# An account of VectorE and GpSimd in a kernel's planner, half-sized GpSimd sums, last divisors on TensorE, a norm in halves

## The chip, the cores and the metric

One Trainium2 chip, one of its cores. The metric is the device time of one execution in microseconds (us), lower is better. TensorE multiplies matrices (PE in the profile; PEld are its weight loads), VectorE (DVE), ScalarE (ACT) and GpSimd (POOL) work on rows of 128 partitions, and SyncE (SP) issues most DMAs. Each engine runs its own instructions strictly in the order in which the program lists them, and waits at an instruction until the semaphores that it names have been raised. So the order of the list is the schedule.

## The reference

Four images of 256 channels and 48 by 48 pixels, all float32. Two layers, each added to its input:

```
x = x + proj(attention(qkv(relu(batchnorm(conv3x3(groupnorm(x)))))))        # 8 heads of 32, 2304 tokens
g = groupnorm(x)
w = conv3x3(g) -> 45 maps; softmax over each 9            # 5 dilations x 9 taps
cat = [g] + [sum over taps k of shift(g, d, k) * w[d, k]  for d in (1, 6, 12, 24, 36)]
x = x + batchnorm over all images (conv1x1(cat))
```

## The kernel before

The images are handled one after the other, in stages that alternate.

**Attention** of image b (`attention`, L1268): nine units of 512 queries (the ninth takes the last 256 queries of both halves of the heads), each in 18 steps of 128 keys. In a step TensorE makes the scores of four heads (`scores`), ScalarE takes their exponent into p, TensorE multiplies p with v into `num` (`weigh`, L1310), and VectorE adds p to `acc` (L1340). Steps in LENT lend three quarters of that sum to a GpSimd-queued DMA that adds into `extra`, which lies in `ring`; L1347 adds `extra` to `acc`. At a unit's end `close` (L1360) makes the divisors: `sums` (L1352) multiplies `acc` with ones on TensorE into `den`, VectorE transposes, takes reciprocals, transposes back and multiplies into `ao` (L1367 to L1377). For the ninth unit nothing follows that could hide it.

**The mixed stage** after it does the second layer of image b (`dynamic_filters`, L1431) and the convolution and q, k, v of image b+1 (`conv_qkv` with `conv_blocks`, L1071) side by side. First `project` (L1407) multiplies `ao` into `pp` and adds it to the image in `pad`; then come the group norm's statistics, and the norm of the whole image: one half of the channels on VectorE (L641), one on ScalarE (L1963). Then these streams run:

- the filters: TensorE makes the 45 maps `pg`, softmax runs over them (`weights`, L1478), and they go out to HBM by DMA and come back in two layouts;
- `near` (L1724), dilation 1, for six chunks c of 384 pixels: nine times ScalarE brings a map into PSUM (`wb`), VectorE multiplies it with the shifted image (`prod`, L1754), and GpSimd adds the product to `near` (L1759), 128x768 at a time;
- `far` (L1585), the other four dilations, as matmuls: VectorE builds a matrix `amat` by predicated copies (L1648, L1660), TensorE multiplies it with the transposed image into two PSUM banks, three times a chunk, and ScalarE or VectorE takes these out, whichever `moved` (L1459) finds less loaded;
- `mixes` (L1809), the 1x1 convolution `py` of all that, chunk by chunk;
- `other`, the convolution of the next image as a Winograd scheme along both axes: GpSimd makes the transformed inputs in `Blocks` (L951: `sum`, `stage0`, `rest`, `along`), TensorE multiplies (`pc`, L1139), and ScalarE, VectorE and GpSimd combine the results; sums with both inputs in SBUF go to VectorE or GpSimd as `either` (L1062) decides. After it come q, k (`pq`) and v (`pv`).

The order of all that is found while the program is written out: `Clock` (L692) keeps a time for each engine, each step adds its assumed cost to it, and `drive` (L1918) takes the first stream whose due time has come by the clock of TensorE, or else a piece of `other`. So a changed cost in the clock changes the order of the instructions on all engines, and which engine gets a sum. What the chip does is not asked.

After attention of the fourth image the second layer has no convolution beside it; there `other` is `late` (L1869), two chunks of the third image that were put off, and the outputs' end (`finish`, L2037).

Of the kernel before, what the change touches and what calls it, by code (L numbers as in the profile page):

```python
# [8 lines left out]
F32 = mybir.dt.float32  # L9
# [48 lines left out]
def conv_preact_kernel(  # L58
# [487 lines left out]
    with tc.tile_pool(name="w", bufs=1) as wpool, tc.tile_pool(  # L546
# [145 lines left out]
        class Clock:  # L692
# [3 lines left out]
            def __init__(self):  # L696
                self.t = dict.fromkeys(("PE", "DVE", "ACT", "POOL"), 0.0)

            def __call__(self, engine, ns, *after):

                self.t[engine] = max(self.t[engine], *(a + 150.0 for a in after), 0.0) + ns
                return self.t[engine]

# [247 lines left out]
        class Blocks:  # L951
# [28 lines left out]
            def sum(self, out, x, y, op):  # L980
                nc.gpsimd.tensor_tensor(out, x, y, op)
                return clock("POOL", 2800)

            def stage0(self):
# [3 lines left out]
                nc.scalar.mul(v[5], d[1], 4.0)  # L988
                self.sum(v[0], d[4], v[0], ALU.subtract)
# [11 lines left out]
            def rest(self):  # L1001
# [3 lines left out]
                for out, x, y, op in (  # L1005
                    (3, d[4], d[2], ALU.subtract), (6, v[6], v[4], ALU.subtract),
                    (4, v[3], v[6], ALU.subtract), (3, v[3], v[6], ALU.add),
                ):
                    yield room
                    end = self.sum(v[out], x, y, op)  # L1010
# [51 lines left out]
        def either(out, a, c, op, *after):  # L1062

            part = 0.5 if len(out.shape) == 2 and out.shape[-1] == XN else 1.0
            if clock.t["POOL"] + 1400 * part <= clock.t["DVE"] + 1000 * part:
                nc.gpsimd.tensor_tensor(out, a, c, op)
                return clock("POOL", 1400 * part, *after)
            nc.vector.tensor_tensor(out, a, c, op)
            return clock("DVE", 1000 * part, *after)

        def conv_blocks(b, psum_tile, blocks, pool, hid):  # L1071
# [23 lines left out]
            def before(i, o):  # L1095

                s12, d12, s34, d34 = (blocks.held[:, j, o] for j in range(4))
                if i == 0:
                    t = spare.pop(0)
                    axpy(t, s34, -4.0, s12)  # L1100
                    relu(o, 2, t, clock("DVE", 700))
                    either(s12, s12, s34, ALU.subtract)
                elif i == 5:
                    t = spare.pop(0)
                    axpy(t, d34, -2.0, d12)
                    relu(o, 1, t, clock("DVE", 700))
                    axpy(d12, d34, -8.0, d12)
                    clock("DVE", 700)
# [159 lines left out]
        def attention(b, q, k_, vT, pools, spare, project, scratch, following):  # L1268
# [41 lines left out]
            def weigh(u, m, p):  # L1310
# [21 lines left out]
                if end and m == NT - 1:  # L1332
                    sums(u, p, True, False)
# [11 lines left out]
                if u and m == (NT - 3 if end else NT - 1):  # L1345
# [6 lines left out]
            def sums(u, rhs, start, stop):  # L1352
                if start:
                    state[u]["den"] = three(f"den_{b}_{u}")[:, 0, :]
                for j, r in enumerate(heads):
# [4 lines left out]
            def close(u):  # L1360

                sums(u, state[u]["acc"], u < last, True)
                if u == last and b == B - 1:
# [18 lines left out]
            for i, (u, m) in enumerate(steps):  # L1382
# [10 lines left out]
                if m == 6 and (u % NH == 1 or u == last):  # L1393
                    while (chunk + 1) * CH <= units[u if u == last else u - 1][0][1]:
                        pp = three(f"pp_{b}_{chunk}")
                        if spare:
# [10 lines left out]
        def project(b, c, ao, pp, norm):  # L1407

            t = pads[b % 2]
            for o in range(NH):  # L1410
                for g in range(NH):
                    nc.tensor.matmul(
                        pp[:, o, :CH],
# [5 lines left out]
            for o in range(NH):  # L1419
                x1 = inside(t, o, c * R, R)  # L1420
                nc.vector.scalar_tensor_tensor(
                    out=x1, in0=rows_of(pp[:, o, :CH]), scalar=pbias[:, o : o + 1], in1=x1,
# [8 lines left out]
        def dynamic_filters(b, ao, chunk, norm, other, pools):  # L1431
# [27 lines left out]
            def moved(dst, src, size, *after, slow=1.0):  # L1459

                if clock.t["ACT"] <= clock.t["DVE"]:
                    nc.scalar.copy(dst, src)  # L1462
                    return clock("ACT", 180 + 0.83 * slow * size, *after)
                nc.vector.tensor_copy(dst, src)
                return clock("DVE", 160 + 1.04 * slow * size, *after)
# [4 lines left out]
            for t in (lg, bmat, amat):  # L1470
                nc.gpsimd.memset(t, 0.0)
# [6 lines left out]
            def weights(cs):  # L1478

                c, pair = cs[0], len(cs) == 2  # L1480
                pg = misc(f"pg_{b}_{c}")
# [58 lines left out]
                yield clock("DVE", 1100 if pair else 320) + 150  # L1540
# [44 lines left out]
            def far():  # L1585

                for c in range(NCK):
# [8 lines left out]
                    for h in range(NH):  # L1596
# [6 lines left out]
                            slow=1.9,  # L1603
                        ))
# [52 lines left out]
                    rowsof = bmat.rearrange("p a (n y) x -> p (a n) y x", y=3)  # L1657
                    for t in range(3):
                        yield lambda: clock.t["DVE"] - AHEAD
# [9 lines left out]
                        end = clock("DVE", 1060)  # L1669
# [54 lines left out]
            def near():  # L1724

                for number, (c, k) in enumerate(sent):
# [32 lines left out]
                    nc.gpsimd.tensor_tensor(cat, cat, prod, ALU.add)  # L1759
                    end = clock("POOL", 1800, end)  # L1760
# [190 lines left out]
            while chunk < NCK:  # L1951
                project(b, chunk, ao, ps_y.tile([P, 2, 512], F32, tag="y", name=f"pp_{b}_{chunk}"), norm)
# [5 lines left out]
            table(AF.Exp)  # L1958
            norm.shift_of()
            for h in range(NH):  # L1960
                t = inside(gn, h)
                if h:
# [415 lines left out]
```

## Time and profile before

| | us |
|---|---|
| median of 3 runs | 2768.17 (2763.59 to 2770.75) |
| the profiled execution | 2768.08 |
| its span, first to last instruction | 2766.3 |

Of the span TensorE is busy 94%, VectorE 77%, ScalarE 65%, GpSimd 27%. By stage, from the busy time in windows of the trace:

| stage, us from the start | length | PE busy | DVE busy | ACT busy | POOL busy |
|---|---|---|---|---|---|
| first convolution, 0 to 152 | 152 | 127.0 | 101.9 | 64.8 | 49.7 |
| attention, four times (the first: 152 to 519) | 367 | 362.1 | 323.4 | 321.7 | 30.9 |
| mixed stage of image 0, 519 to 819 | 300 | 276.6 | 198.8 | 119.5 | 158.6 |
| mixed stage of image 1, 1186 to 1487 | 301 | 278.8 | 195.7 | 119.4 | 158.5 |
| mixed stage of image 2, 1858 to 2132 | 274 | 248.2 | 195.5 | 116.2 | 162.9 |
| last stage, 2502 to 2766 | 264 | 213.9 | 154.6 | 94.7 | 88.5 |

In the lines of the timeline below, the columns are start (us from the span's start), duration (us), engine, line of the kernel, operation, out<-in, shape, count; in brackets the engine's idle time before it and what ended that.

### The profile page before, as it was taken

The numbers are of one execution on the slowest core, as the hardware profiler recorded it, in microseconds if no ns is written. First come the engines' busy times: TensorE is split into PE (matmuls) and PEld (weight loads), VectorE is DVE, ScalarE is ACT, GpSimd is POOL, SyncE is SP. The second block draws the span as 40 slices with busy tenths as digits, with TensorE's granted clock in tenths as the row PEclk, the third lists the DMA queues.
The fourth block names the chain that finished last, engine by engine and source line by source line (L and its number), as shares of the span: only waits on it lengthen the run. The fifth ranks groups of instructions, "written<-read, shape, count | busy, mean of one in ns | idle before, by whom it ended". The sixth has DMA issues, their size and how long they took to land. (4 is left out here: it accounts for less than half of the span.)

```text
span 2766.3 us, 42026 instructions
## 1 busy us (share of the span) xinstructions
PE 2596.0 (94%) x16820; PEld 1089.6 (39%) x16820; DVE 2142.2 (77%) x2045; ACT 1796.7 (65%) x2242; POOL 741.7 (27%) x641
## 2 busy tenths in 40 slices
PE   6999999889999999988999999998999999999994
PEld 5632222455562222345554222244555222234452
DVE  7778888777739988858765988885876988885476
ACT  3478888633449988843346888883445988873244
POOL 5200100456420100065550001016654010000352
PEclk9999999999999999999999999999999999999997
DMA  4704444323242444422333444442335344442465
GB/s 172 219 18 98 109 98 103 81 69 99 78 92 58 105 99 95 109 77 76 89 70 67 92 98 102 99 94 71 86 83 133 93 93 100 94 92 63 118 180 183
DMA packets 135979, 273.64 MB, mean 99 GB/s; under 512 B 56040, under 2 KB 97936, under 8 KB 134880
## 3 DMA queue, kind: packets, MB, share of 16 engines
q0 software_dynamic: 25952, 135.74, 21.5%
q1 hardware_dynamic: 109824, 135.14, 18.4%
q8 instruction: 134, 2.20, 0.4%
q14 instruction: 69, 0.57, 0.1%
HBM read 112.12 MB, written 36.04 MB: 54 GB/s over the span
## 5 line engine op out<-in xcount | busy, mean ns | idle before, releaser
L1340 DVE TENSOR_TENSOR acc<-acc,p 128x2048 f32<-128x2048 f32 (+1 forms) x572 | 1061.2, 1855 | 122.7 <-ACT p L1304 73.1
L1304 ACT ACTIVATE p<-se 128x1536 f32<-128x1536 f32 x648 | 938.7, 1449 | 0.1
L1295 PE MATMUL so<-q,k 32*128 32x512 f32 (+1 forms) x1440 | 726.4, 592 | 19.6 <-ACT p L1303 18.9
L1295 PE MATMUL se<-q,k 32*128 32x512 f32 (+1 forms) x4320 | 735.0, 592 | 0.0
L1324 PE MATMUL num<-p,vT 128*32 128x512 f32 (+1 forms) x5760 | 706.2, 560 | 4.6 <-ACT p L1304 2.4
L1303 ACT ACTIVATE p<-so 128x512 f32<-128x512 f32 x648 | 388.4, 599 | 193.8 <-PE se L1295 82.8
L1759 POOL TENSOR_TENSOR near<-near,prod 128x768 f32<-128x768 f32 x192 | 351.8, 1833 | 357.2 <-DVE prod L1754 347.6
L1295 PEld LDWEIGHTS so<-q,k 32*128 32x128 f32 x1440 | 216.1, 183 | 535.0 <-ACT p L1303 496.3
L1324 PEld LDWEIGHTS num<-p,vT 128*32 128x32 f32 x5760 | 134.5, 108 | 479.2 <-issue 444.3
L1344 POOL DMA_DIRECT2D ring<-p x124 | 105.5, 851 | 779.8 <-ACT p L1304 464.8
L1754 DVE TENSOR_TENSOR prod<-wb,pad 128x768 f32<-128x768 f32 x192 | 181.7, 953 | 68.5 <-ACT wb L1741 48.9
L1854 PE MATMUL py<-far,wsc 128*128 128x384 f32 x704 | 234.5, 487 | 0.0
L1295 PEld LDWEIGHTS se<-q,k 32*128 32x128 f32 x4320 | 226.7, 183 | 5.4 <-ACT p L1304 4.1
L1741 ACT COPY wb<-ws 128x384 f32<-128x384 f32 x216 | 109.0, 509 | 174.7 <-DVE prod L1754 146.4
L1462 ACT COPY far<-far 128x512 f32<-128x512 f32 x92 | 97.4, 1105 | 143.4 <-PE far L1688 142.0
L1342 POOL DMA_DIRECT2D ring<-p x32 | 17.9, 558 | 640.8 <-ACT p L1304 481.5
L1854 PEld LDWEIGHTS py<-far,wsc 128*128 128x128 f32 x704 | 131.9, 190 | 89.8 <-issue 1.8
L1489 PE MATMUL pg<-pad,wcat 128*45 128x384 f32 x864 | 151.7, 498 | 3.5 <-ACT lg L1547 2.1
L1219 PE MATMUL pq<-hid,wqkv 128*128 128x384 f32 x384 | 130.2, 497 | 7.6 <-ACT hid L1089 5.4
L1688 PE MATMUL far<-amat,xT 64*128 64x256 f32 x576 | 86.0, 416 | 18.3 <-DVE amat L1660 18.3
L1219 PEld LDWEIGHTS pq<-hid,wqkv 128*128 128x128 f32 x384 | 73.6, 194 | 60.6 <-ACT hid L1089 7.0
L1340 DVE TENSOR_TENSOR acc<-p,p 128x2048 f32<-128x2048 f32 x36 | 82.3, 2285 | 19.6 <-ACT p L1304 19.6
(305 smaller groups left out, 2711.1 us busy)
## 6 DMA issues: line engine op xcount, KB each, us to landing
ring<-p POOLq DMA_DIRECT2D x156, 768.0 KB, 5.7
ws<-w_d SPq DMA_DIRECT2D x216, 192.0 KB
ring<-u_d SPq DMA_DIRECT2D x36, 512.0 KB
pad<-in_x SPq DMA_DIRECT2D x14, 1152.0 KB
xst<-in_x POOLq DMA_DIRECT2D x36, 192.0 KB, 3.6
x_d<-pad SPq DMA_DIRECT2D x36, 192.0 KB
u_d<-pad SPq DMA_DIRECT2D x12, 512.0 KB
y_d<-y SPq DMA_DIRECT2D x14, 384.0 KB
```

Of the source, the lines that this page charges most:

```text
L1219: nc.tensor.matmul(pq[:, :CH], wqkv[:, i, s, g * P : (g + 1) * P], hid[:, i, cols], start=(i == 0), stop=(i == NH - 1),)
L1295: nc.tensor.matmul(dst[:, at : at + n], k_[r, g, m * P : (m + 1) * P], q[r, g, q0 : q0 + n], start=True, stop=True,)
L1303: nc.scalar.activation(p[:, 0, :], s1, AF.Exp, scale=QS)
L1304: nc.scalar.activation(p[:, 1:, :], s3, AF.Exp, scale=QS)
L1324: nc.tensor.matmul(st["num"][r, at : at + n], vT[:, m, g * P + j * D : g * P + (j + 1) * D], p[:, j, at : at + n], start=(m == 0 and not s ...
L1340: nc.vector.tensor_tensor(st["acc"][:, js], other[:, js], p[:, js], ALU.add)
L1344: nc.gpsimd.dma_start(out=extra, in_=p[:, 1:], accum_op=ALU.add)
L1489: nc.tensor.matmul(pg[64 * s : 64 * s + NG, :CH], wcat[:, ii, k, :], shifted(ii, cc, k // 3 - 1, k % 3 - 1), start=(i == 0 and k == 0), st ...
L1741: nc.scalar.copy(pw[:, :CH], fetched[c, k][0])
L1754: nc.vector.tensor_tensor(prod.rearrange("p h (r w) -> p h r w", w=WW), wb, src, ALU.mult)
L1759: nc.gpsimd.tensor_tensor(cat, cat, prod, ALU.add)
L1854: nc.tensor.matmul(py[c][:, o, :CH], wsc[:, n * NH + i, o * P : (o + 1) * P], rhs, start=(n == 0 and i == 0), stop=(n == order[-1] and i = ...
```

## The change

- `Clock` gets an account of sums: it remembers when GpSimd's recorded work runs, `both` books a VectorE instruction that reads two SBUF operands so that it starts when the GpSimd instruction running then has ended and pushes later GpSimd work back, and `alone` gives that start without booking. `either`, the predicated copies of `amat`, the softmax's last product, the convolution's `axpy` and the copy of `own` use it, with other costs (a sum of 128x576: GpSimd 1300 and VectorE 900 instead of 1400 and 1000). The due time between the three copies of `amat` goes: they follow each other.
- GpSimd's sums of `Blocks` and of `near` are made in halves, one for each half of the channels: 128x600 and 128x384 instead of 128x1200 and 128x768.
- `stage0` gets a sum that stood in `rest`: v3 = d4 - d2, now first of all.
- The ninth unit's divisors: VectorE's last two sums (L1347, and L1340 for step 16) go. In step 16 TensorE adds p, `acc` and `extra` into `den` by 11 matmuls, in step 17 p by four. Five matmuls without use (`busy`) follow in each of the four attentions; before, they stood in the last one alone.
- `lg`, `bmat`, `amat` are cleared by VectorE instead of GpSimd.
- The norm after `project` is made in two halves of 24 rows, with 900 ns of `other` by the clock between them; the exponential's table is loaded in `weights` of chunk 0 instead of before the norm.
- In the last stage `pp` lies in two single banks of the pool `k`, not in the double bank of the pool `y`.

In the built program the number of instructions on TensorE grows by 43 (15 warm, 28 for the divisors); 14 copies out of the far banks go from VectorE to ScalarE (92 and 52 before, 106 and 38 after); in the three mixed stages together TensorE's order, VectorE's and GpSimd's differ in most places from the first chunk on.

```diff
 class Clock:
     def __call__(self, engine, ns, *after):
-        self.t[engine] = max(self.t[engine], *(a + 150.0 for a in after), 0.0) + ns
+        at = max(self.t[engine], *(a + 150.0 for a in after), 0.0)
+        if engine == "POOL":
+            if self.held[0] <= at < self.held[1]:
+                at = self.held[1]
+            self.sums = self.sums[-40:] + [(at, at + ns)]
+        self.t[engine] = at + ns
         return self.t[engine]
+    def alone(self, *after):
+        at = max(self.t["DVE"], *(a + 150.0 for a in after), 0.0)
+        return next((end for start, end in self.sums if start <= at < end), at)
+    def both(self, ns, *after):
+        at = self.alone(*after)
+        self.t["DVE"] = at + ns
+        self.held = at, at + ns
+        if any(start >= at for start, end in self.sums):
+            self.sums = [(start + ns, end + ns) if start >= at else (start, end)
+                         for start, end in self.sums]
+            self.t["POOL"] += ns
+        return self.t["DVE"]
...
 def sum(self, out, x, y, op):
-    nc.gpsimd.tensor_tensor(out, x, y, op)
-    return clock("POOL", 2800)
+    for h in range(NH):
+        nc.gpsimd.tensor_tensor(out[:, h], x[:, h], y[:, h], op)
+        end = clock("POOL", 1400)
+    return end
 def stage0(self):
...
+    self.sum(v[3], d[4], d[2], ALU.subtract)
     self.sum(v[0], d[4], v[0], ALU.subtract)
...
 def either(out, a, c, op, *after):
-    if clock.t["POOL"] + 1400 * part <= clock.t["DVE"] + 1000 * part:
+    if clock.t["POOL"] + 1300 * part <= clock.alone(*after) + 900 * part:
...
-    return clock("DVE", 1000 * part, *after)
+    return clock.both(900 * part, *after)
...
 def weigh(u, m, p):
...
-    if end and m == NT - 1:
-        sums(u, p, True, False)
+    if end and m >= NT - 2:
+        sums(u, p, m == NT - 2, m == NT - 1)
+        if m == NT - 2:
+            sums(u, state[u]["acc"], False, False)
+            sums(u, extra, False, False, 1)
...
-    if u and m == (NT - 3 if end else NT - 1):
+    if u and m == NT - 1 and not end:
         nc.vector.tensor_tensor(rest, rest, extra, ALU.add)
 def close(u):
-    sums(u, state[u]["acc"], u < last, True)
-    if u == last and b == B - 1:
+    if u < last:
+        sums(u, state[u]["acc"], True, True)
+    else:
         busy(ps_a.tile([P, 512], F32, tag="one", name="warm"), 5)
...
 for t in (lg, bmat, amat):
-    nc.gpsimd.memset(t, 0.0)
+    nc.vector.memset(t, 0.0)
...
+    yield lambda: clock.t["DVE"] - AHEAD
     for t in range(3):
-        yield lambda: clock.t["DVE"] - AHEAD
         nc.vector.copy_predicated(amat, ...)
-        end = clock("DVE", 1060)
+        end = clock.both(1060)
...
-    nc.gpsimd.tensor_tensor(cat, cat, prod, ALU.add)
-    end = clock("POOL", 1800, end)
+    for h in range(NH):
+        nc.gpsimd.tensor_tensor(cat[:, h], cat[:, h], prod[:, h], ALU.add)
+        end = clock("POOL", 920, end)
...
-table(AF.Exp)
 norm.shift_of()
-for h in range(NH):
-    t = inside(gn, h)
+for part in range(2):
+    for h in range(NH):
+        t = inside(gn, h, HH // 2 * part, HH // 2)
...
-run(2500)
+    run((900, 1600)[part])
```

## The prediction

> **What bounds the kernel now.** I read the page's first part, then busy time in windows for each stage, then TensorE's waits in one mixed stage, then the timeline. TensorE is busy 94% of the span. In windows of the first mixed stage and of the last stage (window, length, then busy us with instruction counts for PE, PEld, DVE, ACT, POOL, then clock, DMA share, GB/s):
>
> ```profile
> 519.00:819.00 300.00, 276.63 (x1214) 163.37 (x1210) 198.84 (x256) 119.49 (x207) 158.57 (x94) 0.98 0.34 84
> 2502.00:2766.00 264.00, 213.88 (x952) 114.92 (x944) 154.61 (x219) 94.70 (x142) 88.54 (x51) 0.92 0.46 139
> ```
>
> No other engine is full there, so a mixed stage lasts as long as TensorE's work and the waits in it: 23.4, 22.2 and 25.8 us idle in the three. The waits of 519 to 819 (waiting instruction, releaser, then sum, count, mean):
>
> ```profile
> PE far L1688 <- DVE amat L1660: 6.1, 1, 6.1
> PE pc L1139 <- ACT one L1154: 2.9, 1, 2.9
> PE pp L1412 <- DVE ao L1377: 2.8, 1, 2.8
> PE xa L1608 <- ACT own L1462: 2.4, 4, 1.2
> PE xa L1608 <- DVE own L1464: 2.4, 1, 2.4
> PE py L1854 <- POOL near L1759: 1.5, 1, 1.5
> PE den L1356 <- DVE acc L1340: 1.3, 1, 1.3
> ```
>
> The largest comes from sums that exclude each other:
>
> ```profile
> 578.87 3.03 POOL L981 TENSOR_TENSOR cv_q<-pad,cv_q 128x1200 f32<-128x1200 f32 x1
> 579.56 2.95 DVE L1068 TENSOR_TENSOR cv_v<-cv_q,cv_v 128x576 f32<-128x576 f32 x1
> ...
> 582.44 2.96 DVE L1068 TENSOR_TENSOR two<-one,two 128x288 f32<-128x288 f32 x1
> 585.32 1.00 DVE L1660 COPY_PREDICATED amat<-along_y,bmat 128x768 f32<-128x768 uint32 x1
> 586.37 2.08 PE L1688 MATMUL far<-amat,xT 64*128 64x256 f32 x8 [6.10 <-DVE amat L1660]
> ```
>
> A 128x288 sum that takes 0.45 us at its shortest takes 2.96 beside a GpSimd sum of 3 us; four such stand ahead of the third copy of `amat`. After attention the other waits follow:
>
> ```profile
> 524.42 1.06 PE L1356 MATMUL den<-acc,ones 128*32 128x512 f32 x8 [1.33 <-DVE acc L1340]
> 528.24 4.51 PE L1412 MATMUL pp<-ao,wp 128*128 128x384 f32 x8 [2.75 <-DVE ao L1377]
> 533.33 4.12 PE L1139 MATMUL pc<-cv_v,ring 128*128 128x288 f32 x14 [0.58 <-POOL cv_v L1057]
> 543.47 1.72 PE L1139 MATMUL pc<-cv_v,ring 128*128 128x288 f32 x6 [2.92 <-ACT one L1154]
> ```
>
> And in the last stage:
>
> ```profile
> 2509.75 2.82 PE L1412 MATMUL pp<-ao,wp 128*128 128x384 f32 x8 [0.40 <-DVE ao L1377]
> 2514.50 5.16 PE L1881 MATMUL pl<-pad,wsc 128*128 128x384 f32 x10 [1.93 <-issue]
> 2577.30 0.88 PE L1638 MATMUL wT<-ident,wq 36*64 36x36 f32 x12 [2.21 <-DMA wq<-w_d]
> ```
>
> **What the Trainium skill says.** "SBUF — State Buffer", "Who interferes with whom": a VectorE instruction with two SBUF inputs and a GpSimd instruction that reads SBUF shut each other out for the whole instruction. The trace agrees (0.45 against 2.96 us). "TensorE: Matmul & The Clock Gate", "What's actually happening": after an idle window the clock is half, until TensorE has been busy some 3.4 us. The trace agrees: the same eight pp matmuls take 4.51 us in the first stage, 5.46 in the second, 2.82 in the last, which has the five warm matmuls. "Perfetto Trace Analysis", "GPSIMD Engine Instruction": spans on GpSimd are rough; so I take spacing where I can: five near sums start within 9.40 us, 1.88 each. "VectorE: DVE Perf Modes", "Zero memsets can be issued as uint32 (trn2)": a memset takes a cycle per element; at 0.96 GHz, which that page states too, the 1440 elements of lg, bmat, amat give an estimate of 1.5 us. No memset on VectorE is in the trace of before.
>
> **The change, part by part.** Sums against the profiled 2768.08 us (span 2766.3, 1.8 around it); the median of the runs is 2768.17, no correction.
>
> *Divisors.* After 519.09 TensorE would run six sets of four 32-row matmuls, 0.87 us each (num 16; den from p 16, from acc, from extra; num 17; den from p 17): done at 524.3, transposes from 524.5 where they now start at 525.55. So 1.0 us earlier in stages 1 and 2; 0.5 in stage 3 and 0.1 in the last, where p 17 itself comes later. VectorE loses 1.76 + 2.29 us. No new wait: acc of step 15 was ready at 520.18, extra long before.
>
> *Warm.* The five matmuls lie in the idle time before pp (2.75 us). pp falls from 4.51 and 5.46 to 2.82, but the next pc waits for GpSimd anyway (0.58 us at 533.33, and the wait grows by what pp gains). By itself worth about nothing; it makes GpSimd the bound of this spot.
>
> *GpSimd's start.* v3 = d4 - d2 needs only pad, whose readers end with the last scores at 519.2; its first half can run before 522. The next sums are now shut out by VectorE's L1340 until 524.4; without it they start near 522.8. The memsets leave GpSimd (1.5 us) for VectorE's idle time before pp, 4.75 us long, which covers them; uncovered they would cost pp 1.5 us. Neither v3 nor the memsets issue a DMA; on GpSimd's queue they pass only one another. First pc at about 531.4 instead of 533.33: -1.9 us in each mixed stage.
>
> *Norm in halves, table load moved.* Now ScalarE loads the table (1.28 us at 539.43), then norms 2304 elements (2.30 us from 540.84), and `one` queues behind it; TensorE resumes at 543.47 after 2.92 us. With the load gone and half a norm first, `one` comes near 539.1 and TensorE resumes near 539.6: 3.9 us earlier, of which 1.9 are counted above, so -2.0. The table load goes ahead of chunk 0's exponent, beside the 12 pg matmuls and convolution; cover ample. If ScalarE's second half then delays the next copy, I lose up to 1.15 us of it.
>
> *far.* With the account, VectorE's sums stand clear of GpSimd's, which are half as long (1200 elements now 2.52 us unblocked), and the three copies are adjacent. The 6.1 us wait goes; so does the slow clock behind it (far 2.08 us against 1.14 elsewhere, and the next group: -1.6). Back come 0.5 (a rest of the wait) and 1.5: the second far group now follows the first at once, both copied out by ScalarE at 1.1 us each, with two banks. Sum -5.7. The three copies together (3 us) hold up `prod` and sums behind them, whose users are not next on TensorE.
>
> *Later waits in the stage.* xa behind `own` 2.4 + 2.4, near 1.5: 6.3 us. All are sums or copies delayed in the same way; the order changes too widely to follow each, so I take 40%, -2.4, with ends of 0 and -6.
>
> *GpSimd halves.* From 576 and 288 elements unblocked (1.14, 0.79 us) a line gives 0.44 us fixed + 1.22 ns an element: 0.91 for 384. A pair is 1.82 to 2.24 us (the whole's 1.80 and one more fixed part); I take 1.88 against 1.83, +2.4 us on 48 near sums. GpSimd is busy 158 of 300 us, so it is hidden.
>
> *Sum of a mixed stage:* -1.0 - 1.9 - 2.0 - 5.7 - 2.4 = -13.0, less 1.0 since part of the divisors' gain is the same as GpSimd's start: -12.0 in the first two. In the third another -2.7 (half of the 5.4 us that pq waits for hid) and +2.0, as one far group now stands at its very end, after all of v, ahead of attention's first scores: -12.7.
>
> *Last stage:* divisors -0.1; pp in bank k, so pl no longer waits for y's release -1.9; norm and pg -0.6; the wT wait for the DMA is covered, since chunk 2's 30 pg matmuls now stand there, -2.2. The wait of pf for okay (3.5 us) stays. -4.8.
>
> Total -12.0 - 12.0 - 12.7 - 4.8 = -41.5: 2768.1 - 41.5 = 2727 us.
>
> **Rivals.**
> - *Only the ends gain* (0.17): the far banks' copies and near's later place take the far gain back. For: ScalarE takes 14 more far copies of 1.1 us. Against: ScalarE is busy 119 of 300 us. Then 3 x 3.9 + 4.8 = 16.5: 2752.
> - *Nearly all waits go* (0.08): 22 us a stage less 4 for what can't go, and 8 in the last: 3 x 18 + 8 = 62 less, 2706.
> - *No net change* (0.06): the new order shifts the waits as much as it cuts. For: 43 instructions more on TensorE and an order found without the chip. Then 2765.
> - *Slower* (0.10): halves on GpSimd cost well over half. Place: the near chain, which ends in py's wait (1.5 us now). At 1.2 us a half, a pair is 2.4, 0.57 more on 48 sums in four stages, 109 us, half of it exposed as `near` comes late for py: +55 - 41 = +14, 2782. It decides from a pair of 2.26 us (41 / (4 x 48 x 0.5) = 0.43 over 1.83), just over my upper bound.
>
> **How the numbers follow.** Main case 0.59, own range 2706 to 2746 (-6 and +2 on the later waits in each stage, far between -8 and -2). The range 2700 to 2760 takes in the second case and nearly the third, and leaves out the last two and tails, under 0.2. A measurement of this kernel can tell about 0.3% (8 us) from no change: faster 0.84, same 0.06, slower 0.10.
>
> **What would show it.** In the profile after: transposes about 1 us earlier against attention's end; pp near 2.8 us in all four; far's wait for amat under 1 us; the longest 128x288 sum on VectorE well under 2.96 us; a near half near 0.94 us; TensorE idle some 12 us a mixed stage instead of 22 to 26; no wait of pl after pp. Wrong if near pairs exceed 2.2 us, if py waits for near or far for its banks, or if VectorE's sums are as long as before.

## The result and the profile after

| | before | changed | ratio |
|---|---|---|---|
| median of 10 runs, us | 2768.49 | 2759.41 (2751.31 to 2770.28) | 0.9968 (0.9957 to 0.9978) |
| 22 more runs of the changed kernel, 39 of before | 2766.18 | 2759.34 (2751.27 to 2776.74) | 0.9980 (0.9968 to 0.9991) |

The kernel became faster by some 6 to 9 us where 41 had been forecast. It also scatters more: 19 us over ten runs against 7. The profiled execution took 2758.79 us (span 2756.9). By stage, in us of the traces: an attention runs from its first scores (the products of q and k) to its last, a mixed stage from there to the next attention's first scores. The second execution is that of a later experiment. Its stages differ from those of the first by up to 6 us, so a smaller difference in one stage of one run says little.

| stage | forecast, change | before | changed | changed, second execution |
|---|---|---|---|---|
| first mixed stage | -12.0 | 300.0 | 294.1 | 295.3 |
| second | -12.0 | 301.2 | 295.1 | 301.2 |
| third | -12.7 | 273.8 | 268.8 | 271.5 |
| fourth attention | 0 | 369.4 | 385.6 | 386.1 |
| last stage | -4.8 | 264.7 | 257.2 | 256.4 |
| first convolution and attentions 1 to 3 | 0 | 1257.2 | 1256.1 | 1252.4 |

So half of the gain in the mixed stages is missing in the first execution, four fifths in the second. The fourth attention takes 16 us more in both; what differs there is its start. The windows of the first mixed and the last stage in the changed kernel, columns as in the prediction:

```profile
516.12:810.24 294.12, 277.57 (x1236) 165.11 (x1235) 182.97 (x251) 121.76 (x209) 174.10 (x157) 0.99 0.33 82
2499.74:2756.90 257.16, 211.88 (x970) 115.16 (x970) 146.77 (x218) 98.67 (x147) 93.83 (x96) 0.93 0.47 143
```

The waits of TensorE in the first mixed stage of the changed kernel (sum, times, longest):

```profile
PE pg L1526 <- ACT lg L1584: 3.0, 2, 2.2
PE pc L1166 <- DVE two L1192: 2.7, 2, 1.5
PE pc L1166 <- POOL cv_v L1084: 2.4, 1, 2.4
PE pc L1166 <- ACT one L1181: 2.2, 2, 1.9
PE xa L1646 <- ACT own L1494: 2.0, 3, 0.7
PE xa L1646 <- DVE own L1496: 1.5, 2, 1.0
PE far L1726 <- ACT far L1494: 1.4, 2, 1.2
```

The wait of far for amat (6.1 us) is gone, as is den's for acc. (In the second execution far waits 1.5 us for amat in the second and third mixed stages.) What far waits for now is the copy out of its banks, 1.4 us. Other waits have grown: pc's for GpSimd ahead of the first pc from 0.6 to 2.4 us, pg's for lg from 0.9 to 3.0, and pc's for `two` on VectorE, absent before, is 2.7. The longest of VectorE's sums of this shape is shorter, 1.68 us instead of 2.96; the median is not (line of `either`, before and changed, min/median/max in ns):

```profile
L1068 DVE TENSOR_TENSOR two<-one,two x25: 448/1049/2959, 574.5 to 1989.7; 128x288 f32<-128x288 f32 x25
L1095 DVE TENSOR_TENSOR two<-one,two x30: 436/1136/1683, 561.2 to 2029.8; 128x288 f32<-128x288 f32 x30
```

The start of that stage, attention's last scores ending at 516.12, in the timeline of the changed kernel:

```profile
516.32 3.64 POOL L1006 TENSOR_TENSOR cv_k<-pad 128x600 f32<-128x600 f32 x2 [9.33 <-issue]
519.91 5.31 POOL L1006 TENSOR_TENSOR cv_q<-pad,cv_q 128x600 f32<-128x600 f32 x4
...
524.16 2.82 PE L1444 MATMUL pp<-ao,wp 128*128 128x384 f32 x8 [0.39 <-DVE ao L1408]
...
529.33 4.14 PE L1166 MATMUL pc<-cv_v,ring 128*128 128x288 f32 x14 [2.35 <-POOL cv_v L1084]
...
538.48 1.24 PE L1166 MATMUL pc<-cv_v,ring 128*128 128x288 f32 x4 [1.92 <-ACT one L1181]
540.89 0.91 PE L1166 MATMUL pc<-cv_v,ring 128*128 128x288 f32 x2 [1.17 <-DVE two L1192]
541.73 3.64 PE L1526 MATMUL pg<-pad,wcat 128*45 128x384 f32 x12
```

pp comes 8.0 us after attention's end (before: 9.1) and is short. The first pc comes after 13.2 us (before: 14.2): v3, now first, takes 3.6 us, so that the sums which the first pc needs start 3.8 us after attention's end; before it was 3.1, but there VectorE's last sum of `acc` held them up. The norm has two waits, 1.9 and 1.2 us, in place of one of 2.9, and the clock falls behind them: twelve pg take 3.64 us, before 2.17. pg starts 25.6 us after attention's end, before 26.0. In the second execution the slow clock hits the first fourteen pc instead (5.67 us, here 4.14), and pg starts after 26.6 us. So by the end of these twelve pg nothing is left of the earlier start: 29.2 and 28.8 us after attention's end in the two executions, before 28.2 (second stage 29.9 and 30.0, before 30.2; third 28.8 and 30.0, before 27.6).

The fourth attention begins so (changed kernel, the lines of four engines put in order of time):

```profile
2116.82 5.75 POOL L1798 TENSOR_TENSOR near<-near,prod 128x384 f32<-128x384 f32 x6 [0.33 <-DVE prod L1792]
2119.97 2.08 PE L1322 MATMUL se<-q,k 32*128 32x512 f32 x6 [4.56 <-DVE prod L1792]
2122.59 0.33 SPq L1864 DMA_DIRECT2D late_d<-near  x1
2123.03 0.37 SPq L1865 DMA_DIRECT2D late_d<-far  x1
2129.95 0.60 ACT L1330 ACTIVATE p<-so 128x512 f32<-128x512 f32 x1 [11.18 <-DMA late_d<-far]
2130.60 1.22 PE L1322 MATMUL so<-q,k 32*128 32x512 f32 x1 [8.54 <-ACT p L1330]
```

The same in the kernel before:

```profile
2125.77 0.33 SPq L1825 DMA_DIRECT2D late_d<-near  x1
2126.21 0.37 SPq L1826 DMA_DIRECT2D late_d<-far  x1
...
2132.13 1.12 PE L1295 MATMUL so<-q,k 32*128 32x512 f32 x2
2133.34 0.60 ACT L1303 ACTIVATE p<-so 128x512 f32<-128x512 f32 x1 [0.63 <-PE so L1295]
```

Of the third image, chunks 5 and 4 are put off to the last stage: own, near and far go to HBM (`late_d`) on SyncE's queue, in this order, when near and far are both done. The first p of the next attention takes over the memory that they lay in. far's 1.5 MB take 6.9 us from issue to the release of p. Before, the store was issued 5.9 us ahead of attention's first scores; with the same 6.9 us (an estimate from the changed kernel's trace) it would have landed 0.2 us ahead of the first p, just in time. Now TensorE arrives 18.0 us sooner (2114.10 against 2132.13), but near is done only 3.2 us sooner. Two waits, 4.6 us of se for the bank that near's last map lay in and 8.5 of so for p, and a slow clock behind them (granted 0.82 in the first 56 us of this attention, before 1.00) make up the 16 us. Counted from attention's end, near's last sum even comes later: 277.3 us against 267.4.

### The profile page after: what moved, and what is told of

It reads as the page before. It is cut to its first block, busy times and chain, and to the rows that moved or that the text cites. A ratio compares the mean times of both kernels' runs of the same rounds, so it can differ in the third digit from the quotient of the medians.

```text
span 2756.9 us, 42411 instructions
## 1 busy us (share of the span) xinstructions
PE 2602.5 (94%) x16906; PEld 1097.9 (40%) x16906; DVE 2090.5 (76%) x2030; ACT 1807.9 (66%) x2251; POOL 790.0 (29%) x871
## 3 DMA queue, kind: packets, MB, share of 16 engines
q1 hardware_dynamic: 109824, 135.14, 18.3%
## 5 line engine op out<-in xcount | busy, mean ns | idle before, releaser
L1798 POOL TENSOR_TENSOR near<-near,prod 128x384 f32<-128x384 f32 x384 | 389.5, 1045 | 344.7 <-DVE prod L1792 342.9
L1494 ACT COPY far<-far 128x512 f32<-128x512 f32 x106 | 110.3, 1109 | 91.5 <-PE far L1726 91.5
L1526 PEld LDWEIGHTS pg<-pad,wcat 128*45 128x45 f32 x864 | 54.6, 122 | 96.0 <-issue 82.4
```

The source lines that it names most:

```text
L1526: nc.tensor.matmul(pg[64 * s : 64 * s + NG, :CH], wcat[:, ii, k, :], shifted(ii, cc, k // 3 - 1, k % 3 - 1), start=(i == 0 and k == 0), st ...
L1798: nc.gpsimd.tensor_tensor(cat[:, h], cat[:, h], prod[:, h], ALU.add)
```

## The experiments

Ratios are to the kernel before on the same chip, with 95% intervals. What separates a run from the changed kernel is the difference of two such ratios (the changed kernel's were 0.9968 and 0.9980), so it is uncertain by some 5 us. Stage lengths are those of one execution each. Diffs are against the changed kernel if nothing else is said, and shortened.

### The fourth attention

**far_first**

```diff
-own, near, far stored, in this order
+far stored, then own, near                # SyncE's queue, chunks 5 and 4 of the third image
```


> The changed kernel with one edit: of chunks 5 and 4 of the third image, put off to the last stage, the far sums go out to HBM ahead of the copy of the image and of the near sums, where before they stood behind them on SyncE's queue. Theory A (the start of the fourth attention waits for the chain near sums, then near's store, then far's store, whose buffers attention's p takes over): far's 1.5 MB start some 7 us earlier and no longer end 7 us after the last near sum, p's first write comes 4 to 6 us earlier, so 2759 falls to about 2754 (4 to 6 us less than the changed kernel). Rival B (the start is held by the last far groups and their copies on ScalarE, or by the bank of the last map): no gain, within 1 us.

Measured 0.9952 (0.9936 to 0.9968), 2756.85 us: 4.4 us less than the changed kernel, by the ratios alone not clear of noise. The trace shows the gain where it was expected: p now waits for near's store, its wait falls from 8.5 to 4.0 us, and the bank's stays (4.8 after 4.6). Theory A.

**near5_cut**

```diff
+left_out = b == B - 2 and c == NCK - 1 and not centre      # no wb, prod, near sums then; clock as before
 ...
```


> The changed kernel, order of everything else kept; left out are eight of the nine taps of near of chunk 5 of the third image (their copies into PSUM, products and GpSimd sums). Theory A: the near chain of that chunk ends some 20 us earlier, the fourth attention starts without its two waits of 4.6 and 8.5 us and the slow clock behind them: 2759 falls by 13 to 17 us, to about 2744. Rival B (far's last groups, or attention itself is slower): the gain is only what 8 products and 16 sums beside TensorE cost, under 3 us.

Measured 0.9922 (0.9910 to 0.9935), 2751.01 us: 12.7 us less, just under what theory A expected. The kernel leaves out part of the sum, so its time is a probe only. The fourth attention takes 377.5 us, 8 less, and the third stage 263.5, 5 less. The bank's wait is gone, but 5.5 us for p stay: far's last group itself ends with the stage, and its store takes 7 us. So near is the larger part and far's place a second.

**no_account**

```diff
 def alone(self, *after):
-    return next((end for start, end in self.sums if start <= at < end), at)
+    return at
 def both(self, ns, *after):
-    ...
+    return self("DVE", ns, *after)
```


> The changed kernel with the account of sums off: VectorE's sums are booked as other work, GpSimd's bookings are not pushed back; new costs, halves and all other parts stay. Theory A (the account fills VectorE in the plan, so near, which is due when VectorE is within 2.5 us, comes later): near's chunk 5 in the third image ends some 10 us earlier against attention's end, the fourth attention's wait shrinks to under 4 us; but sums shut each other out again, 3 to 5 us more TensorE waits in each of three mixed stages, so about the same time, 2755 to 2765. Rival C (the account is what gains in the mixed stages and near's lateness comes from the halves): 2770 or more, near's chunk 5 as late as in the changed kernel.

Measured 0.9966 (0.9954 to 0.9978), as the changed kernel. Mixed stages 300.7, 303.7 and 276.8 us, 7 to 9 longer than in the changed kernel's first execution; fourth attention 370.0, 16 shorter; near's last sum 267.4 us after attention's end. So the account gains 23 us in the mixed stages against the first execution of the changed kernel, 13 against the second (of TensorE's idle time there it takes away 13 to 14 us against both), and loses 16 behind the third. For near and the attention theory A holds.

**acc_not_b2**

```diff
+clock.on = b != B - 2          # alone and both as in no_account while it is off
```


> The changed kernel with the account of sums off in the stage of the third image alone, the other stages as in the changed kernel. Theory A (the account gains 6 to 9 us in each mixed stage, but in the third it puts near later and the chain near, store, first p of the fourth attention gives back 16): that stage gets about 8 us longer, the fourth attention 13 to 16 us shorter, so 6 to 8 us less than the changed kernel, ratio to before 0.994 to 0.995. Rival B (the fourth attention is late for far's last groups, which come late with or without the account): the stage longer by 8 us and attention shorter by under 5, 3 us or more slower than the changed kernel, ratio 0.998 or above.

Measured 0.9948 (0.9934 to 0.9962), 2752.78 us. The third stage takes 277.6 us (8.8 more), the fourth attention 368.9 (16.7 less). The chain in its trace, to be held against the changed kernel's above:

```profile
2113.38 0.33 SPq L1869 DMA_DIRECT2D late_d<-near  x1
2113.82 0.37 SPq L1870 DMA_DIRECT2D late_d<-far  x1
...
2122.80 1.12 PE L1327 MATMUL so<-q,k 32*128 32x512 f32 x2
...
2124.00 0.60 ACT L1335 ACTIVATE p<-so 128x512 f32<-128x512 f32 x1 [0.63 <-PE so L1327]
```

The store is issued 9 us ahead of the scores, and p waits for TensorE alone. Theory A. Why the account makes near late is read from the code and was not tested by itself: it books VectorE's waits for GpSimd, VectorE's clock runs ahead of TensorE's, and near's steps are due only when it is within 2.5 us. In the changed kernel GpSimd's first sum of near's third chunk starts 155 us after attention's end, with the account off 146.

**split_acc**: as acc_not_b2, and far of chunks 5 and 4 stored as soon as it is done, without waiting for near.

> The changed kernel with the account off in the third image's stage alone, and there the far sums of chunks 5 and 4 are stored as soon as they are there, without waiting for near. Theory A (without the account near is done some 9 us ahead of the stage's end, and the fourth attention waits for nothing): as the kernel with the account off there, ratio 0.9948, within 3 us, since the fourth attention there had no wait left to take away. If the stage also gets shorter as far's last groups come 27 us earlier, up to 3 us less: 0.9935.

Measured 0.9965 (0.9953 to 0.9977), 2759.45 us: a miss, 5 us over acc_not_b2 where at most 3 were expected, though the two intervals overlap. The profiled execution has no such wait at the fourth attention (368.7 us) and a last stage of 261.1 us, 3 longer than there. Whether the moved stores or the scatter told of below cause the rest stays open.

### The halves

**whole_sums**

```diff
-for h in range(NH): nc.gpsimd.tensor_tensor(out[:, h], ...)    # 1400 each; near: 920 each
+nc.gpsimd.tensor_tensor(out, x, y, op)                         # 2800;      near: 1800
```


> The changed kernel with GpSimd's sums whole again (128x1200 and 128x768, planned at 2.8 and 1.8 us), account and all else kept. Theory A (halves let a blocked VectorE sum wait 1.5 us instead of 3, worth 3 to 4 us in each mixed stage, and cost GpSimd 0.14 to 0.2 us a pair off the path, but 7 us of near chain in the third): mixed stages 2 to 5 us longer; the longest VectorE sum about 2.5 us; the whole 5 to 10 us slower than the changed kernel, ratio 0.998 to 1.001. Rival G (halves cost more than they bring, near gets late through them): near's chunk 5 ends 8 to 10 us earlier in the third image, the whole 5 us or more faster than the changed kernel.

Measured 1.0048 (1.0035 to 1.0061), 2778.23 us: 19 to 22 us slower than the changed kernel, more than expected; of the theories A is the nearer, and rival G falls: near's last sum in the third stage comes 275.5 us after attention's end, hardly earlier than the 277.3 of the changed kernel. Mixed stages 303.6, 303.6 and 274.9 us, fourth attention 376.9. VectorE's sums reach 3.3 us again, and single waits of 2.6 to 3.1 us come back (far for amat, wT for xT, pq for hid). In this plan the account without the halves does not pay: the kernel with neither, and the old costs (ends_only, below), came out at 1.0005. The halves cost little: an undisturbed near pair takes 1.95 us against 1.81.

### The start of the mixed stages

**ends_only**: the kernel before with the parts that touch neither account, costs nor halves (divisors, warm, v3 first, memsets, norm, pp banks).

> The kernel before with only the parts that don't touch the account, the costs or the halves: divisors on TensorE with warm matmuls, v3 first, memsets on VectorE, norm in halves with the table load later, pp in single banks in the last stage. The prediction gave these parts 3.9 to 4.9 us in each mixed stage and 4.8 in the last, 16.5 in all: 2752. What the changed kernel's trace shows (60 us after attention's end, TensorE's useful work is 3 us behind, GpSimd is busy without a gap there) says that little of it is kept in the mixed stages and 5 to 7 us in the last: 2760 to 2764.

Measured 1.0005 (0.9997 to 1.0013): less than even the smaller expectation. The last stage gained 3.3 us; the mixed ones lost 5.0, 4.4 and 6.5. pg starts 24.9 us after attention's end, 1.1 sooner; later pq waits 3.6 us for hid, a wait that the first two stages of the kernel before do not have. TensorE's idle time in the three stages, 22.5, 23.3 and 26.4 us, is what it was before (23.4, 22.2, 25.8), although 3.7 us of new matmuls a stage fill some of it. v3's place had changed the order of the whole stage.

**ends_v3_old**: the same with v3 in its old place; TensorE's order in the mixed stages is then that of the kernel before (their traces have the same sequence).

> The kernel before with divisors, warm matmuls, memsets, norm in halves with the later table load, and pp in single banks in the last stage; v3 in its old place, costs, account and halves as before, so the mixed stages keep the order of the kernel before. The prediction's steps (less GpSimd's start by v3) give 1.0 + 2.0 in two mixed stages, 2.5 in the third and 4.8 in the last: 13 us less, ratio 0.995. Theory L (the start's gain is there but ends at wT of chunk 0, which waits for its weights from HBM, and at GpSimd, so that 0 to 1.5 us a stage are kept, and 5 to 8 in the last): 5 to 12 us less, ratio 0.9955 to 0.998. If the mixed stages show nothing at all: 0.998 or above.

Measured 0.9966 (0.9955 to 0.9976), 2760.10 us: as much as the whole change. But not in the mixed stages: 302.4, 300.5 and 275.9 us against 300.0, 301.2 and 273.8. The last stage takes 258.7, 6.0 less. Theory L. Of the rest, 4.9 us lie ahead of the first mixed stage and in attentions 1 to 3, where the two executions of the changed kernel differ by 3.7; what they are stays open. TensorE's waits, attention's end at 517.03:

```profile
525.07 2.82 PE L1441 MATMUL pp<-ao,wp 128*128 128x384 f32 x8 [0.39 <-DVE ao L1405]
529.27 4.14 PE L1163 MATMUL pc<-cv_v,ring 128*128 128x288 f32 x14 [1.39 <-POOL cv_v L1081]
538.30 1.24 PE L1163 MATMUL pc<-cv_v,ring 128*128 128x288 f32 x4 [1.79 <-ACT one L1178]
540.71 0.98 PE L1163 MATMUL pc<-cv_v,ring 128*128 128x288 f32 x2 [1.17 <-DVE two L1189]
541.62 3.56 PE L1523 MATMUL pg<-pad,wcat 128*45 128x384 f32 x12
...
568.53 0.90 PE L1672 MATMUL wT<-ident,wq 36*64 36x36 f32 x12 [2.06 <-DMA wq<-w_d]
```

The first pc comes 1.9 us sooner than before, pg 1.4 sooner; then pg runs on a slow clock, wT waits 2.1 us for chunk 0's weights from HBM (before: 0.7), and comes 51.5 us after attention's end, where it was 50.3.

**no_ends**: all these parts undone in the first three attentions and mixed stages.

> The changed kernel with the parts at the ends undone in the first three attentions and mixed stages: divisors by VectorE's sums again, no warm matmuls, v3 in its old place, memsets on GpSimd, norm whole with the table load ahead of it; account and halves stay, and the last attention and stage keep all of it. Theory H (these parts cost more than they bring in a mixed stage: 3.7 us more TensorE work, first pc only 1 us earlier, chunk 0's weights later; the kernel with them alone had mixed stages 5 us longer than before): mixed stages up to 5 us shorter than the changed kernel's, 8 to 15 us less in all, ratio 0.991 to 0.994. Rival I (they gain about 1 us at the start of each stage and the rest of what the kernel with them alone lost is the order that the plan happens to find): within 5 us of the changed kernel on either side, 0.995 to 0.9985. The prediction's own figure (3.9 to 4.9 us gained a stage): 12 to 15 us more, ratio 1.001 or above.

Measured 1.0081 (1.0068 to 1.0094), 2791.94 us: 31 us slower than the changed kernel, far more than any of the expectations. Its first mixed stage has one wait of 11.2 us, for a sum on VectorE, that none of the runs above has, and the three mixed stages last 311.2, 313.4 and 284.1 us.

**v3_old**

```diff
 def stage0(self):
-    self.sum(v[3], d[4], d[2], ALU.subtract)
 ...                                                # in rest:
+    (3, d[4], d[2], ALU.subtract), (6, v[6], v[4], ALU.subtract),
```


> The changed kernel with v3 in its old place alone. Theory J (v3's place changes the plan, and the order found with it has a wait of 11 us of TensorE for a convolution sum behind three copies of amat on VectorE, in each of three mixed stages; this is all of what the kernel with the ends undone lost): mixed stages 308 to 313 us again with one wait of about 11 us, the whole 25 to 33 us slower than the changed kernel, ratio 1.006 to 1.009. Rival (the loss came from the other parts undone): within 8 us of the changed kernel, no such wait.

Measured 1.0077 (1.0061 to 1.0092), 2787.92 us; mixed stages 312.5, 314.0 and 284.9 us; theory J. Its longest waits in the first mixed stage:

```profile
PE pc L1165 <- DVE pad L1094: 11.2, 1, 11.2
PE pg L1525 <- ACT lg L1583: 3.0, 2, 2.1
```

A sum that this pc needs stands on VectorE behind a row of sums and three copies of amat. TensorE's order in the mixed stages is that of no_ends, so the long wait there has the same cause. One GpSimd sum at another place in the plan is worth 27 us: not by its 3.6 us, but by the order that the plan finds.

**no_ends_v3**: as no_ends, with v3 kept first; TensorE's order in the mixed stages is then that of the changed kernel.

> The changed kernel with divisors, warm matmuls, memsets and norm as before in the first three attentions and mixed stages, v3 first as in the changed kernel. The plan of the mixed stages is then that of the changed kernel, so this is the worth of these parts by themselves. The prediction's steps (1.0 for the divisors and 2.0 for the norm a stage) give 7 to 9 us slower than the changed kernel, ratio 1.000; theory H (GpSimd's chain bounds the first 15 us, and clock falls in the waits behind): within 3 us of the changed kernel, ratio 0.996 to 0.998, pg of the first chunk within 1 us of 25.6 us after attention's end.

Measured 1.0025 (1.0016 to 1.0034), 2774.24 us: 12 (by the ratios) to 15 us (by the medians) slower than the changed kernel on the same chip, more than either theory. Mixed stages 299.6, 304.6 and 270.2 us. The trace shows where: v3, first, meets VectorE's last sums of attention, which are back.

```profile
518.86 5.09 POOL L1006 TENSOR_TENSOR cv_k<-pad 128x600 f32<-128x600 f32 x2 [9.34 <-issue]
...
519.71 2.92 DVE L1379 TENSOR_TENSOR acc<-acc,ring 128x1536 f32<-128x1536 f32 x1
...
522.73 3.37 DVE L1372 TENSOR_TENSOR acc<-acc,p 128x2048 f32<-128x2048 f32 x1
...
526.15 1.91 PE L1388 MATMUL den<-acc,ones 128*32 128x512 f32 x8 [3.56 <-DVE acc L1372]
```

They take 2.92 and 3.37 us where they took 1.76 and 2.29, and pp comes 12.1 us after attention's end, pg 30.4 (25.6 in the changed kernel). So v3 first needs the divisors on TensorE, which make room for it.

**old_norm**: the norm whole again, table load ahead of it.

> The changed kernel with the norm as before: whole, the table for the exponent loaded ahead of it, no load in the weights of chunk 0. The prediction gave halves and later load 2.0 us a mixed stage and 0.6 in the last, which undone would cost 6 to 7 us: ratio 0.999. Theory F (in the trace of the changed kernel the waits behind the norm are 1.9 + 1.2 us where they were 2.9, and the weights of chunk 0 come 1 to 2.4 us later since the load now stands ahead of their exponent and the plan charges 1.5 us for it): within 3 us of the changed kernel, and wT of chunk 0 about 2 us earlier.

Measured 0.9972 (0.9958 to 0.9986), 2761.07 us: within 3 us of the changed kernel, theory F for the time. wT did not come sooner (55.8 us after attention's end in this execution), so that part of it fell.

**no_warm**

```diff
-else:
+elif b == B - 1:
     busy(...)
```


> The changed kernel without the five warm matmuls in the first three attentions (the last keeps them); the plan is the same. Theory D (GpSimd's inputs are what the first pc waits for, so the warm clock of pp only lengthens that wait, and the clock falls in it anyway): pp takes 4.5 us or more again, the wait of 2.35 us ahead of the first pc falls to about 0.5, first pc at the same time within 0.3 us, the whole within 2 us of the changed kernel. Rival E (a warm pp brings its additions and statistics forward and these the norm): each mixed stage 1.5 to 2.5 us longer, 5 to 7 us in all.

Measured 0.9977 (0.9967 to 0.9986), 2762.18 us: 2 to 3 us slower than the changed kernel's first runs, equal to its later ones; not told apart. Rival E (5 to 7 us) falls. Theory D was wrong in a detail: pp took 2.82 us in the first stage, warm without warm matmuls (4.33 and 4.51 in the other two). There the fourteen pc behind it ran slowly, 5.37 us against 4.14; but they do so with the warm matmuls too, in the second execution of the changed kernel (5.67), so this is not what the missing five cost.

### The clock

**after_again**: the changed kernel once more.

> The changed kernel once more. Ratio 0.9968 within 0.0015. If the scatter of its time (19 us in ten runs against 7 of the kernel before) is the clock after short waits, a second profile shows the same waits in the first mixed stage but other slices with a clock under 1, and that stage between 294 and 300 us.

Measured 0.9980 (0.9968 to 0.9991). In the second mixed stage the waits over 0.3 us add up to 15.8 us in the first execution and 16.0 in this one, and the stage took 295.1 and 301.2 us. TensorE was busy 279.0 and 284.8 us of it with the same number of instructions, so the difference is in how fast they ran. Two windows of that stage, 180 to 240 us after attention's end, first execution, then second:

```profile
1360.80:1390.80 30.00, 27.36 (x107) 16.87 (x106) 23.49 (x30) 15.18 (x25) 15.36 (x15) 1.00 0.24 62
1390.80:1420.80 30.00, 30.00 (x102) 17.48 (x101) 20.92 (x30) 13.04 (x26) 16.73 (x19) 1.00 0.36 80
```

```profile
1360.20:1390.20 30.00, 29.69 (x112) 18.12 (x110) 20.42 (x25) 11.34 (x21) 14.40 (x14) 0.89 0.21 61
1390.20:1420.20 30.00, 27.68 (x93) 16.53 (x94) 21.82 (x35) 16.00 (x29) 12.80 (x13) 0.94 0.27 65
```

The waits are the same in sum; where the granted clock is lower, 0.89 and 0.94 against 1.00, the stage is longer.

**keep_warm_b2** (in spite of its label, the account is on in every stage)

```diff
 project(b, chunk, ao, pp, norm)
+busy(misc(...), 5)                                 # in the mixed stages only, as the two below
 ...
 norm.shift_of()
+busy(misc(...), 4)
 ...                                                # between the halves of the norm
+busy(misc(...), 2)
```


> The changed kernel with eleven more warm matmuls in each mixed stage: five behind pp, ahead of the first pc's wait of 2.35 us; four ahead of the norm, two between its halves, where waits of 1.9 and 1.2 us stand. Theory K (the clock falls after these waits and costs 1 to 2 us behind them, as where twelve pg took 3.64 us against 2.16): these matmuls fit into the waits, pg's first twelve take 2.2 us, each mixed stage 1 to 2 us shorter, 3 to 6 us in all, ratio 0.995 to 0.996. Rival: the clock there is full in most executions, and the matmuls only add: same or up to 4 us slower, ratio 0.997 to 0.998.

Measured 0.9954 (0.9937 to 0.9971), 2752.52 us: 6.8 us less than the changed kernel on that chip, with intervals that just overlap. The trace is as theory K has it. Waits of 2.35, 1.92 and 1.17 us are down to 0.2, 0.25 and 0.3, and pg's first twelve take 2.17 us in the first stage, 2.16 and 2.17 in the other two:

```profile
529.26 2.32 PE L1293 MATMUL warma<-wsc,ident 128*128 128x256 f32 x10
531.77 4.14 PE L1166 MATMUL pc<-cv_v,ring 128*128 128x288 f32 x14 [0.18 <-POOL cv_v L1084]
...
543.98 2.17 PE L1526 MATMUL pg<-pad,wcat 128*45 128x384 f32 x12
```

**best**: acc_not_b2 and these warm matmuls.

> The changed kernel with the account off in the third image's stage and with eleven more warm matmuls at the start of each mixed stage. If the two causes are separate, their gains add (5 to 6 and 5 to 7 us against the changed kernel): ratio 0.992 to 0.9945, 2744 to 2751. If the warm matmuls gained only by what the fourth attention gives back or loses: no better than either, 0.9945 to 0.996.

Measured 0.9926 (0.9904 to 0.9949), 2748.58 us against 2767.82: within the noise the gains add, and it is faster than both kernels.

## Why the prediction was wrong, step by step

Two terms carry most of the miss of some 32 us. The start of a mixed stage was to bring 3.9 us in each of three, and hardly any of it was left when the first twelve pg had ended; and the end of the third stage, put at +2.0, cost 16 us in the attention behind it. The rest is waits that the new order brought and the sum had no term for.

- **Divisors, -1.0:** right. pp came 8.0 instead of 9.1 us after attention's end.
- **Warm, nothing by itself:** not refuted; without the five the time changed by no more than 3 us. That they make pp fast is true of two stages in three (no_warm).
- **GpSimd's start, -1.9 together with the divisors:** half, 1.0. With the old place of v3 the first pc did come 1.9 us sooner, 12.2 us after attention's end (ends_v3_old). The step let v3 run in free time, but it stands ahead of the sums that this pc needs, and lasts 3.6 us: with it 12.7 (ends_only and whole_sums). It also left out that these sums are longer in halves: with both 13.2. The memsets had no part in it; on GpSimd they stood behind the sums of the first pc.
- **Norm, -2.0:** failed. With the two items above pg was to start 3.9 us sooner; it started 0.4 us sooner in one execution and 0.6 later in the other. One wait of 2.9 became two of 1.9 and 1.2, and a slow clock, at pg or at the first pc, took 1.5 us. The whole norm (old_norm) costs no more than 3 us over the whole kernel. What ends_v3_old kept of the start in the first stage (1.4 us at pg) ended in the slow clock of pg and at wT's wait for the DMA. The prediction had not asked what would be late next on this path: there, chunk 0's weights.
- **far, -5.7:** about right. TensorE's idle time ahead of far fell from 18.3 to 5.7 us over the whole kernel, 4.2 a mixed stage (3.0 in the second execution), before any effect on the clock; without the clock's 1.6 the term was 4.1. (Ahead of the third copy stood five VectorE sums, of 1.05, 2.24, 1.16, 2.95 and 2.96 us, not four as long as the last.)
- **Later waits, -2.4:** right for the waits that it names, wrong in taking them for all. In the first stage xa's fell from 4.8 to 3.5 us and py's of 1.5 went, 2.8 in all. But pg's for lg and pc's for `two` grew by 4.8 us, 1.2 of it the second wait of the norm, and far's for the copy out of its banks by 1.4. In the first stage all idle time fell from 22.1 to 16.2 us (listed waits over 0.3 us), while 3.7 us of TensorE work came in (14 divisor records of 0.11 us and ten warm ones of 0.22). The prediction had some 12 us of idle time.
- **Third stage, +2.0 for a far group at its end:** the largest miss. far's place was seen, its store and p's wait for it were not; near's lateness, which weighs more, was not seen at all. 16 us in place of 2; near5_cut, far_first, no_account and acc_not_b2 show it. That the account is what makes near late is shown; by which step of the planner is argued. The rival on the slower side named the near chain, but by dear halves and at py. An undisturbed pair of halves costs 0.14 us more than the whole, and py did not wait for near.
- **Last stage, -4.8:** right in kind, 7.5 in size. pl's wait right behind pp (1.9 us) is gone, and so are those of pg for the norm (0.8) and of wT for the DMA (2.2). pf's wait for okay, which was to stay, fell from 3.5 to 2.4.

What was missing altogether is that the parts do not add. v3's place is worth 27 us by the order that it brings about, v3 first needs the divisors on TensorE, and the account needed the halves. A price from the profile of before holds for the order of before.

## What to carry to other kernels

When the bound engine gets faster over a stage, look for the chain that ends just in time at the stage's end, stores and the memory they free included: here its slack was 0.2 us, and 16 us went into it. In a kernel whose order is found by a planner, test a part with the order kept, and read what the new order puts last; the sum of single prices says little. Where waits of 1 to 2 us lie close together, warm matmuls in them may pay by the clock behind them: here some 2 us a stage, by runs that are just not clear of noise.

## What the runs showed of the hardware

- The clock behind short waits differs from execution to execution: waits of the same sum (15.8 and 16.0 us) gave stages of 295.1 and 301.2 us, and in the first mixed stage the slow clock lay at pg in one execution and at the first pc in the other. The Trainium skill, "TensorE: Matmul & The Clock Gate", "What's actually happening", says that the window in which activity is counted runs freely, so that the moment of a change depends on where in it the work falls. These runs agree with that, but no run here shows the window itself. The changed kernel scatters more than the one before (19 us against 7 over ten runs each, 25 over 22 against 15 over 39 in the later runs); that short waits are the reason is not shown.
- VectorE's predicated copies of amat take longer beside GpSimd's sums too: three in a row took 4.94 us while such sums ran, against 3.1 in whole_sums where none did. In the mean of all 72 a copy took 1.18 us in the changed kernel, 1.10 before.
- A store of 1.5 MB held the memory it read for 6.9 us after its issue, and so the next stage's first write (7.0 us in near5_cut).
